# Small additions on GpSimd behind the gathers of adj, and an instruction order made from 16-byte ranges

## The chip, the cores and the metric

The kernel runs on one core of one Trainium2 chip. The metric is the device time of one execution in microseconds (us), as the median over several executions. Beside it there is a profile of one execution, taken by the hardware profiler. Its engines are TensorE (PE; its weight loads are PEld), VectorE (DVE), ScalarE (ACT), GpSimd (POOL) and SyncE (SP), which only issues transfers here.

## What is computed

Two layers of graph attention over 2708 nodes with 256 features. `adj` is 2708 x 2708, sparse, with non-negative entries and a full diagonal. Cut to what matters:

```python
# layer 0: sums over neighbours, three attention heads, two GRU cells
node_support = adj_without_diagonal @ h
edge_output  = gru_cell(node_support, h, edge_weights)
for each of 3 heads:
    hW = h @ W                        # e from sums of hW over the neighbours
    att = softmax over neighbours of e, masked where adj is 0
    edge_support += (att * adj_without_diagonal) @ hW
node_output = gru_cell(edge_support / 3, h, node_weights)
x = layernorm(x + diag * edge_output + diag * node_output)

# layer 1: four heads of 64
h = x @ W
e = leaky_relu(s_src[:, None] + s_dst[None, :]), kept where adj > 0.5
out = (softmax(e, axis=0)) applied to h, + bias
x = layernorm(x + out)
```

## The kernel before

The kernel doesn't multiply by the whole of `adj`. It looks once at all of it and makes lists of the rows in which a block of columns has entries; afterwards it gathers these rows alone.

**Scan (0 to about 200 us).** SP loads `adjT` in three parts of up to 1024 columns, 128 rows at a time. ScalarE takes signs, VectorE the marks of entries over 0.5, and TensorE packs those into bits. For each block of columns (`BLOCKS0`, 51 blocks of 28 to 64 columns) VectorE finds the rows with entries; `listed` turns that into indices `f_idx` through prefix sums on VectorE (arena `f_lists`) and small matmuls (`rk`, `lst`).

**Layer 0 (about 200 to 710 us).** Each block has 1 to 8 listed tiles of 128 rows, 131 in all. For each tile there are two gathers on GpSimd, both indirect DMAs through one column of `f_idx`: one takes the block's entries of these rows from `adjT` in DRAM (`fetch_raw`, into one of 40 slots of `f_raw`; the first 16 go into the space of `f_ah`), the other takes the rows of x with the head weights from the DRAM table `f_T0` (`fetch_rows`, into one of four `f_xg` buffers). Another 22 tiles are whole stretches of rows, which SP loads without a list. VectorE makes the weighted columns `f_four` out of both, TensorE sums into `acc`. Columns are worked in six groups of up to 512 (`CH`), in the order `turn`: 4, 3, 2, 1, 0, 5. When a group is summed, `cells_and_norm` runs its two GRU cells on TensorE (`side`), ScalarE and VectorE, normalises, and writes the table `f_T1` for layer 1. GpSimd adds twice for each block of 128 nodes (`f_xacc`, and the bias into `f_low`).

**Layer 1 (about 714 us to the end).** For the 32 blocks of `BLOCKS1` (96 tiles) GpSimd gathers rows of `f_T1` into the arena `f_lists` (`fetch_h`), VectorE masks and scales them, TensorE sums, and each finished block of 128 nodes is normalised and stored (`finished`). The lists for layer 1 are made by the same `listed`, in the same arena, before.

**What sets the order.** The program's calls are not issued as they are written. Each call goes to an object `Order` (lines 88 to 375), which keeps it as a node, or several calls as one node where `together()` encloses them. `issue` (line 223) finds the dependences: `spans` (line 134) gives, for each operand, the ranges of bytes of a partition that it touches, in cells of 32 bytes (1024 in DRAM, a whole bank in PSUM), and two nodes that touch a common cell, one of them writing, are kept in their order. `duration` (line 180) gives each call a price in us. From these a list scheduler works forwards and backwards twelve times and keeps the order with the shortest planned span. All instructions are then issued from line 375, in that order, so nearly every row of the profile says L375; each engine works its own instructions in the order given. A name that begins with `in_` (an input in DRAM) makes no dependence. The prices and cells are the planner's alone: they change which instruction comes when, not what it does.

Gathers are issued by `gathered` (line 812), from `fetch_raw` (line 841), `fetch_rows` (line 1063) and `fetch_h` (line 1344). A gather has the price 1.36 us in `duration`.

Of the kernel before, what the change touches and what calls it, by code (L numbers as in the profile page):

```python
# [14 lines left out]
U32 = mybir.dt.uint32  # L15
# [7 lines left out]
P = 128  # L23
# [49 lines left out]
def _size(ap):  # L73
    n = 1
    for d in ap.shape[1:]:
        n *= d
    return n


def _width(dt):  # L80
    return {F32: 4, I32: 4, U32: 4, BF16: 2, F16: 2, U16: 2, F8: 1}[dt]
# [6 lines left out]
class Order:  # L88
# [44 lines left out]
    @staticmethod  # L133
    def spans(ap):

        name, pat, wide = ap.tensor.name, [tuple(d) for d in ap.ap], _width(ap.dtype)
        if name.startswith("in_"):
            return name, []
        space = str(ap.space)
        if "PSUM" in space:  # L140
            return name, [(0, 1)]
        if "DRAM" in space:
            at, cell = ap.offset, 1024
        else:
            step = pat[0][0]
            at, cell = (ap.offset % step if step else ap.offset), 32
            pat = pat[1:]
        run, outer = 1, []
        for s, n in sorted((abs(s), n) for s, n in pat if s and n > 1):
            if s <= run + cell // wide:  # L150
                run = s * (n - 1) + run
            else:
                outer.append((s, n))
        starts = [at]
        for s, n in outer:
            starts = [a + k * s for a in starts for k in range(n)]
        out = []
        for a in sorted(starts):
            lo, hi = a * wide // cell, (a + run) * wide - 1
            hi = hi // cell + 1  # L160
            if out and lo <= out[-1][1]:
                out[-1] = (out[-1][0], max(hi, out[-1][1]))
            else:
                out.append((lo, hi))
        return name, out
# [14 lines left out]
    def duration(self, call):  # L180
        engine, method, args, kw = call
        outs, ins = self.touched(call)
        out = outs[0]
        n = max([_size(out)] + [_size(a) for a in ins if method in ("tensor_reduce", "bn_stats")])
        if engine == "tensor":
            moving = kw["rhs"] if method == "matmul" else args[1]
            still = kw["lhsT"] if method == "matmul" else args[1]
            cols = _size(moving) if method == "matmul" else P
            if _width(moving.dtype) == 4:
                if method == "transpose":  # L190
                    return 0.2
                return max(4 * cols + 2 * _size(still), 800 if _size(still) > 96 else 500) / 2400.0
            return max(cols, 108) / 2400.0 + 0.01
        if engine == "vector":
            wide = [a for a in outs + ins if _size(a) > 1]
            fast = all(_width(a.dtype) == 2 for a in wide) or (
                method == "tensor_scalar" and all("PSUM" not in str(a.space) for a in wide)
            )
            if method in ("tensor_tensor_scan",):
                n *= 1.5  # L200
            if method == "reciprocal":
                n *= 8
            if method in ("bn_stats", "tensor_reduce", "memset", "copy_predicated"):
                fast = False
            return ((n / 2 if fast else n) + 150 + (60 if method == "scalar_tensor_tensor" else 0)) / 960.0
        if engine == "scalar":
            extra = sum(isinstance(kw.get(k), bass.AP) for k in ("scale", "bias"))
            return (n + 224 + 93 * extra) / 1200.0
        if engine == "gpsimd":
            if method == "indirect_dma_start":  # L210
                return 1.36
            return (n * (4.0 if method == "tensor_add" else 0.8) + 60) / 960.0
        return 0.45

# [185 lines left out]
def fast_path(ctx: ExitStack, tc: tile.TileContext, i: dict, out: bass.AP, bad: bass.AP):  # L400
    nc = tc.nc
    R = Order(nc)
    V, S, G, T, Q = R.vector, R.scalar, R.gpsimd, R.tensor, R.sync
    x, xT_in, adj, adjT = i["x"], i["xT"], i["adj"], i["adjT"]
# [26 lines left out]
    def home(name, shape, dt=F32):  # L431
        return const.tile(shape, dt, name=name)
# [31 lines left out]
    T0 = dram.tile([N, TW0], F32, name="f_T0")  # L464
    T1 = dram.tile([N, TW1], U32, name="f_T1")
# [52 lines left out]
    G.iota(pos_i, pattern=[[P, NB]], base=0, channel_multiplier=1)  # L518
    spans = sorted({(b[2], NB) for b in BLOCKS0} | {(0, NB)})
    pos = home("f_pos", [P, len(spans), NB])  # L520
    past = home("f_past", [P, 1])
    V.tensor_scalar(past, pid, float(size[last]), 1.0e6, op0=ALU.is_ge, op1=MUL)
    for n, (lo, hi) in enumerate(spans):
        V.tensor_scalar(pos[:, n], pos_i, float(-P * lo), None, op0=ADD)
        if lo:
            V.memset(pos[:, n, :lo], 1.0e6)
        V.tensor_add(pos[:, n, last:], pos[:, n, last:], past)
# [53 lines left out]
    column = ({}, {})  # L581
# [9 lines left out]
    idx = [home(f"f_idx{l}", [P, wide_of[l]], I32) for l in (0, 1)]  # L591
# [7 lines left out]
    for l, blocks in enumerate((BLOCKS0, BLOCKS1)):  # L599
        at = l * slots_of[0]  # L600
# [208 lines left out]

    batch_part = [next(k for k, (lo, hi) in enumerate(parts) if lo <= BLOCKS0[b[0][0]][0] < hi) for b in batch0]  # L810

    def gathered(dst, table, ix, at):
        G.indirect_dma_start(dst, None, table, bass.IndirectOffsetOnAxis(ap=ix, axis=0), element_offset=at)

    work0 = []
    for n, (d0, w, q, room_) in sorted(enumerate(BLOCKS0), key=lambda e: (turn.index(e[1][0] // CH), e[0])):
# [16 lines left out]
    def raw_slots(a, b):  # L833
        if b <= early_n:
            return early[:, a:b]
        return raw_all[:, (a - early_n) % raw_n : (a - early_n) % raw_n + b - a]
# [4 lines left out]
    def fetch_raw():  # L841
        k = fetched[0]
        if k == len(work0):
            return False
        n, whole, t = work0[k]
        d0, w = BLOCKS0[n][:2]
        dst = raw_slots(k, k + 1)[:, 0, :w]
        if whole:
            with R.after(loads[1, 16]):
                Q.dma_start(dst, adjT[t * P : (t + 1) * P, d0 : d0 + w])  # L850
        else:
            gathered(dst, adjT, idx[0][:, column[0][n] + t : column[0][n] + t + 1], d0)
        raw_of[k] = dst
        fetched[0] += 1
        return True

    loads, known, seen = {}, [], []
    for g, (c0, c1) in enumerate(parts):
# [12 lines left out]
        for k in range(NB):  # L871
            p = size[k]
            at = at_ring.next()
# [47 lines left out]
    while fetched[0] < raw_n + early_n:  # L921
        fetch_raw()
# [39 lines left out]
    while s0 < len(BLOCKS1):  # L962
        n0 = by_slot[s0]
        d0, w = BLOCKS1[n0][:2]
# [13 lines left out]
    for c, cell in enumerate(("edge", "node")):  # L978
        pair = []
        for wn in ("Wih", "Whh"):  # L980
            t = wts.take([P, KD, 3 * D])
# [73 lines left out]
    while k < len(work0):  # L1055
        n, whole, t = work0[k]
# [6 lines left out]
    def fetch_rows(j):  # L1063
        ks = pairs0[j]
        n, whole, t = work0[ks[0]]
        if whole:
            return
        xg = xg_ring.next()
        for m, k in enumerate(ks):
            t = work0[k][2]  # L1070
            gathered(xg[:, m, :], T0, idx[0][:, column[0][n] + t : column[0][n] + t + 1], 0)
        rows_of[j] = xg

    def layer0(j):
# [188 lines left out]
    for j in range(ahead - 1):  # L1263
        fetch_rows(j)
    for g in turn:
        spread_dens(g)
        for j in steps[g]:
            if j + ahead - 1 < len(pairs0):
                with R.part(f"rows{BLOCKS0[work0[pairs0[j + ahead - 1][0]][0]][0] // CH}"):
                    fetch_rows(j + ahead - 1)  # L1270
            with R.part(f"sums{g}"):
                layer0(j)
            done = pairs0[j][-1] + 1
            check_raw(done)
            with R.part("raw"):
                while fetched[0] < min(max(checked[0], early_n) + raw_n, len(work0)):
                    fetch_raw()
        cells_and_norm(g)
# [65 lines left out]
    def fetch_h(j):  # L1344
        n, ts = work1[j]
        hg = hg_ring.next()
        for m, t in enumerate(ts):
            c = column[1][n] + t
            gathered(hg[:, m, :].bitcast(U32), T1, idx[1][:, c : c + 1], 0)
        hg_of[j] = hg  # L1350

    outs = {}
# [70 lines left out]
    for j in range(ahead1 - 1):  # L1423
        fetch_h(j)
    for j, (n, ts) in enumerate(work1):
        g = BLOCKS1[n][0] // CH
        if g + 1 < NG and g + 1 not in S_of:
            spread_values(g + 1)
        if j + ahead1 - 1 < len(work1):
            fetch_h(j + ahead1 - 1)  # L1430
        layer1(j)
# [455 lines left out]
```

## Time and profile before

| | us |
|---|---|
| three executions | 840.92, 841.58, 844.88 |
| median | 841.58 |
| the profiled execution, whole | 901.63 |
| its span, first to last instruction | 899.9 |

The profiled execution is slower than the others, so its microseconds are compared with its own total. In its span TensorE is busy 678.9 us, VectorE 551.1, GpSimd 436.2 and ScalarE 233.0. GpSimd's costliest groups:

| gathers | count | busy us | mean ns |
|---|---|---|---|
| adj's entries into `f_raw` | 115 | 116.2 | 1011 |
| adj's entries into `f_ah` (the first 16) | 16 | 16.1 | 1005 |
| rows of `f_T0` into four `f_xg` buffers | 131 | 138.6 | 1058 |
| rows of `f_T1` into `f_lists` | 96 | 108.6 | 1132 |

(The third row adds four groups: 39.1 + 34.7 + 34.7 + 30.1 over 36 + 33 + 32 + 30.) [...]In the profile's rows an arrow gives what is written on its left and read on its right, and "idle before" is the time in which the engine did nothing before an instruction, with what ended it: an engine and tile, a DMA, "issue" (nothing that the profile shows), or "remote", an unknown queue.

### The profile page before, as it was taken

What the parts mean: (1) busy time and instruction counts of PE and PEld (TensorE: products, weight loads), DVE (VectorE), ACT (ScalarE), POOL (GpSimd) and SP (SyncE); (2) the same over time, 40 slices, a digit from 0 to 9 for tenths busy, and PEclk for the clock granted to TensorE, in tenths of its full rate; (3) what the DMA queues carried; (4) which work ended last, traced back from release to release, by engine and by line L of the source; (5) the groups of instructions that cost most, each with busy time, mean ns of one, the idle gap of its engine ahead of it and who ended that gap; (6) DMA issues with size and microseconds to landing.
All of it is one profiled execution on the core that took longest, in us unless ns stands there. A gap on an engine that the chain in (4) does not pass through costs nothing. (4 is left out here: it accounts for less than half of the span.)

```text
span 899.9 us, 12878 instructions
## 1 busy us (share of the span) xinstructions
PE 678.9 (75%) x4588; PEld 481.8 (54%) x4588; DVE 551.1 (61%) x1355; ACT 233.0 (26%) x496; POOL 436.2 (48%) x565
## 2 busy tenths in 40 slices
PE   1474764778769899988898879999988565776664
PEld 1463653565335555565555545564467464765553
DVE  7373576695126847763436644561498734977996
ACT  4403664001011321122111121123125301113244
POOL 7006000476725716666677777550005266777830
PEclk9995555588979999999999999999999855787886
DMA  9934886572101312243223222121004244555541
GB/s 300 335 124 144 280 307 186 164 227 59 23 17 47 120 57 51 44 113 84 51 53 91 81 74 74 51 74 42 1 1 130 106 124 124 175 154 169 159 139 47
DMA packets 60647, 103.50 MB, mean 115 GB/s; under 512 B 20887, under 2 KB 37027, under 8 KB 59935
## 3 DMA queue, kind: packets, MB, share of 16 engines
q1 hardware_dynamic: 40337, 61.41, 20.5%
q0 software_dynamic: 17472, 41.15, 17.6%
q8 instruction: 38, 0.62, 0.3%
q10 hardware_dynamic: 2766, 0.04, 0.2%
q14 instruction: 34, 0.28, 0.1%
HBM read 93.07 MB, written 12.27 MB: 117 GB/s over the span
## 5 line engine op out<-in xcount | busy, mean ns | idle before, releaser
L375 POOL DMA_INDIRECT f_raw<-in_adjT_dram,f_idx x115 | 116.2, 1011 | 47.7 <-issue 31.9
L375 PE MATMUL acc<-f_lists 128*65 128x128 f32 (+3 forms) x768 | 100.3, 303 | 51.7 <-DVE f_lists L375 37.9
L375 POOL DMA_INDIRECT f_lists<-f_T,f_idx x96 | 108.6, 1132 | 50.2 <-issue 20.6
L375 PE MATMUL side<-f_xT,f_wts 128*128 128x512 f32 (+1 forms) x288 | 123.0, 553 | 13.0 <-DVE f_big L375 11.9
L375 PE MATMUL side<-f_big,f_wts 128*128 128x512 f32 (+1 forms) x288 | 123.1, 553 | 9.5 <-ACT f_big L375 8.4
L375 PEld LDWEIGHTS acc<-f_lists 128*65 128x65 f32 x768 | 92.0, 189 | 58.4 <-DVE f_lists L375 42.6
L375 PEld LDWEIGHTS side<-f_big,f_wts 128*128 128x128 f32 x288 | 53.1, 194 | 64.4 <-issue 54.9
L375 POOL DMA_INDIRECT f_xg__133<-f_T,f_idx x36 | 39.1, 1085 | 99.5 <-DMA f_T<-f_E 71.6
L375 PEld LDWEIGHTS side<-f_xT,f_wts 128*128 128x128 f32 x288 | 51.0, 191 | 60.7 <-issue 43.3
L375 ACT ACTIVATE f_big<-f_wts 128x1024 fp8e4<-128x1024 f32 (+2 forms) x66 | 61.7, 952 | 48.3 <-DMA f_wts<-in_adjT_dram 39.8
L375 POOL TENSOR_TENSOR f_xacc<-f_xacc,f_low 128x256 f32<-128x256 f32 (+1 forms) x22 | 22.6, 1029 | 96.9 <-ACT f_low L375 96.1
L375 ACT ACTIVATE f_big<-side,f_biases 128x512 f32<-128x512 f32 (+1 forms) x48 | 30.4, 636 | 129.3 <-PE side L375 76.6
L375 DVE TENSOR_TENSOR f_big<-f_big 128x512 f32<-128x512 f32 (+1 forms) x48 | 30.4, 636 | 49.7 <-ACT f_big L375 42.8
L375 DVE TENSOR_SCALAR f_wts<-f_wts 128x1024 fp8e4<-128x1024 f32 (+1 forms) x66 | 43.2, 662 | 25.1 <-DMA f_wts<-in_adjT_dram 23.3
L375 PE MATMUL side<-f_big,f_gat_w 128*128 128x512 f32 (+1 forms) x144 | 56.1, 544 | 2.5 <-DVE f_s_d L375 1.6
L375 DVE TENSOR_TENSOR f_lists<-f_big,f_lists 128x512 f32<-128x512 f32 (+4 forms) x56 | 44.3, 791 | 21.3 <-PE acc L375 6.9
L375 PEld LDWEIGHTS <-f_big 128*128 128x128 fp8e4 x968 | 36.4, 103 | 34.2 <-issue 18.6
L375 POOL DMA_INDIRECT f_xg__135<-f_T,f_idx x33 | 34.7, 1052 | 36.9 <-PE acc L375 24.4
L375 PE MATMUL side<-f_pow,f_wts 128*128 128x8 bf16 x484 | 23.6, 170 | 37.1 <-DVE f_wts L375 35.6
L375 PEld LDWEIGHTS <-f_lists 128*32 128x32 f16 (+6 forms) x617 | 35.4, 134 | 27.1 <-DVE f_lists L375 17.2
L375 PE MATMUL lst<-f_lists 128*128 128x256 f16 (+4 forms) x285 | 37.5, 297 | 16.0 <-DVE f_lists L375 16.0
L375 DVE TENSOR_TENSOR f_lists<-f_iota,f_lists 128x2816 f16<-128x2816 f16 (+5 forms) x26 | 49.4, 1922 | 0.3
(244 smaller groups left out, 1208.2 us busy)
## 6 DMA issues: line engine op xcount, KB each, us to landing
f_wts<-in_adjT_dram SPq DMA_DIRECT2D x42, 512.0 KB
f_wts<-in_adjT_dram SPq DMA_DIRECT2D x21, 330.0 KB
f_big<-f_Rd SPq DMA_DIRECT2D x5, 1024.0 KB
f_big<-f_Sd SPq DMA_DIRECT2D x5, 1024.0 KB
f_T<-f_ah SPq DMA_DIRECT2D x21, 132.0 KB
f_X<-f_low SPq DMA_DIRECT2D x21, 128.0 KB
f_low<-f_X SPq DMA_DIRECT2D x21, 128.0 KB
out_dram<-f_big SPq DMA_DIRECT2D x21, 128.0 KB
```

The source lines that it names most:

```text
L375: getattr(getattr(self.nc, engine_), method)(*args, **kw)
```

## The change

There are four edits.

1. A tile `f_idle` of one partition and 128 elements of 4 bytes is made and set to zero. `gathered` puts each gather in a node of its own, and where the table is `adjT` it adds to the same node one addition on GpSimd, `idle + idle` into `idle`. Nothing else reads or writes that tile. The argument `l` that `gathered` now takes isn't used.
2. `spans` makes no dependence from names that begin with `f_idle`, as for inputs.
3. The cells of SBUF from which dependences are found are 16 bytes instead of 32.
4. In `duration` a gather costs 1.27 us instead of 1.36, and the addition 0.45; a gather of adj with its addition is thus one node of 1.72.

```diff
-        if name.startswith("in_"):
+        if name.startswith(("in_", "f_idle")):
             return name, []
...
-            at, cell = (ap.offset % step if step else ap.offset), 32
+            at, cell = (ap.offset % step if step else ap.offset), 16
...
             if method == "indirect_dma_start":
-                return 1.36
+                return 1.27
+            if outs[0].tensor.name.startswith("f_idle"):
+                return 0.45
...
-    def gathered(dst, table, ix, at):
-        G.indirect_dma_start(dst, None, table, bass.IndirectOffsetOnAxis(ap=ix, axis=0), element_offset=at)
+    idle = home("f_idle", [1, P])
+    G.memset(idle, 0.0)
+
+    def gathered(l, dst, table, ix, at):
+        with R.together():
+            G.indirect_dma_start(dst, None, table, bass.IndirectOffsetOnAxis(ap=ix, axis=0), element_offset=at)
+            if table is adjT:
+                for _ in range(1):
+                    G.tensor_add(idle, idle, idle)
...
-            gathered(dst, adjT, idx[0][:, column[0][n] + t : column[0][n] + t + 1], d0)
+            gathered(0, dst, adjT, idx[0][:, column[0][n] + t : column[0][n] + t + 1], d0)
...
-            gathered(xg[:, m, :], T0, idx[0][:, column[0][n] + t : column[0][n] + t + 1], 0)
+            gathered(0, xg[:, m, :], T0, idx[0][:, column[0][n] + t : column[0][n] + t + 1], 0)
...
-            gathered(hg[:, m, :].bitcast(U32), T1, idx[1][:, c : c + 1], 0)
+            gathered(1, hg[:, m, :].bitcast(U32), T1, idx[1][:, c : c + 1], 0)
```

## The prediction

> **What bounds the kernel now.** I read the busy row in slices first, then busy times by stage, then GpSimd's instructions in order of time, and last the chain of waits over the seam between the two layers. The page's slices:
>
> ```profile
> PE   1474764778769899988898879999988565776664
> DVE  7373576695126847763436644561498734977996
> POOL 7006000476725716666677777550005266777830
> ```
>
> Each digit is 22.5 us. TensorE is at 8 or 9 tenths from about 200 to 650 us (layer 0), and at 5 to 7 in layer 1, where VectorE is at 7 to 9. GpSimd looks like 6 or 7 tenths in layer 0, but that row leaves out what lies between its instructions. In order of time:
>
> ```profile
> 466.60 0.95 POOL L375 DMA_INDIRECT f_raw<-in_adjT_dram,f_idx  x1 [0.30 <-issue]
> 467.86 0.95 POOL L375 DMA_INDIRECT f_raw<-in_adjT_dram,f_idx  x1 [0.30 <-issue]
> 469.12 0.95 POOL L375 DMA_INDIRECT f_xg__133<-f_T,f_idx  x1 [0.31 <-issue]
> 470.08 0.73 POOL L375 TENSOR_TENSOR f_xacc<-f_xacc,f_low 128x256 f32<-128x256 f32 x1
> 470.77 1.41 POOL L375 TENSOR_TENSOR f_low<-f_low,f_bias_b 128x256 f32<-128x256 f32 x2
> 472.33 0.96 POOL L375 DMA_INDIRECT f_raw<-in_adjT_dram,f_idx  x1 [0.16 <-issue]
> ```
>
> Columns are start, duration, operation, and in brackets the idle time before it. The reader is to see three prices: a gather is 0.95 us; between two gathers stand 0.30 us; between a gather and an addition 0.01, and between an addition and the next gather 0.16. So a gather really takes 1.25 us of the queue. By stage:
>
> ```profile
> 352.00:470.00 118.00, 103.62 (x428) 65.60 (x427) 59.79 (x150) 23.18 (x56) 79.32 (x80) 0.96 0.27 67
> 470.00:530.00 60.00, 52.87 (x214) 36.26 (x213) 37.73 (x101) 12.30 (x30) 44.57 (x44) 0.94 0.31 81
> 530.00:606.00 76.00, 70.36 (x236) 42.67 (x235) 41.67 (x101) 15.98 (x32) 48.71 (x53) 0.98 0.25 68
> 606.00:714.00 108.00, 94.02 (x523) 59.50 (x521) 65.12 (x136) 37.32 (x88) 16.07 (x15) 0.98 0.17 56
> ```
>
> (busy us of PE, weight loads, DVE, ACT, POOL, then clock and DMA). Between 352 and 530 us TensorE is busy 156.5 of 178 us, GpSimd 123.9; adding the 0.30 us behind each of some 118 gathers makes about 159. Counting only the idle stretches over 0.30 us in the instruction list, less 0.30 each, GpSimd has 19.8 us free there, and 17.1 us between 530 and 606. TensorE and GpSimd are thus nearly balanced. The seam, by the chain of waits:
>
> ```profile
> 714.68 2.07 DVE f_lists L375 x2
> ...
> 717.35 2.54 PE lst L375 x22
> 719.89 1.82 issue
> 721.72 0.15 DVE f_hm L375
> 721.87 5.13 another core or an unknown queue
> ...
> 727.03 0.07 DVE f_idx L375
> ...
> 727.14 0.57 DVE f_lists L375 x2
> ```
>
> The last list of layer 1 is finished while the first gathers of layer 1 are already under way, and VectorE, which works in order, stands 5.13 us at the write of f_idx before the first masks (727.14) can go.
>
> **What the Trainium skill says.** GPSIMD Engine Reference, section 3.1 (elementwise accounting), puts a two-input addition at about 2.6 cycles per element plus a dispatch; the trace's 0.73 us for 256 elements agrees in size. SBUF — State Buffer, section "Who interferes with whom", says that a VectorE instruction with two SBUF inputs and a GpSimd instruction that reads SBUF block each other. The trace agrees: four f_xacc additions that take 0.73 us alone took 8.70 us from 674.47 on, beside VectorE's f_lists work. Perfetto Trace Analysis, section "GPSIMD Engine Instruction", advises timing GpSimd by the spacing of starts; that is done here.
>
> **The idle additions.** There are 131 gathers of adj (115 into f_raw, 16 into f_ah). Each is now followed by an addition of 128 elements on one partition, which no row shows. By the row for 256 elements (0.73 us, of which by the skill's 2.6 cycles at 1.2 GHz 0.55 is elements) I estimate 0.18 + 0.28 = 0.46 us. The step adds 0.01 + 0.46 + 0.16 and loses the 0.30 behind the gather: 0.33 us. Bounds: 0.1 us, if the addition is mostly dispatch like the small memsets (0.10 to 0.17 us: 0.01 + 0.13 + 0.16 - 0.30 is about nothing), and 0.54 us if VectorE blocks it as it does the others (f_xacc means 1.04 and f_low 0.84 against 0.73 and 0.70, so about 0.2 more). I take 0.33: 131 x 0.33 = 43 us of GpSimd. The addition depends on nothing and nothing reads it; the memset of its tile is one of 153. Behind each addition stand the next gathers in GpSimd's queue, and for the gathers of f_xg TensorE waits.
>
> Where this lies: the 17 gathers before 100 us have 71.6 us of idle time behind them (nothing). About 20 between 200 and 250 (7 us) stand before an idle stretch of 14 us at 249 (nothing). From 352 to 530 there are 63 in the list: 63 x 0.33 = 20.8 against 19.8 us free, so 1.0 late; from 530 to 606 there are 11, 3.6 against 17.1, which takes it up. If that cover were gone, 1.0 us would be late; I count +0.5. VectorE's blocked operations cost at most 0.46 us each, and it has idle time in this stage (59.8 busy of 118): nothing.
>
> **The new order.** Every engine's order is made from prices and dependences. The price of a gather falls from 1.36 to 1.27 us; the trace's spacing is 1.25, with means of 1.01 + 0.30 for f_raw and 1.13 + 0.30 for the layer-1 gathers. A gather of adj with its addition is priced 1.72 against my 1.58. So the planner now holds GpSimd to be a little fuller than it is in layer 0 and a little emptier in layer 1; gathers of adj lose rank where something else can go. No instruction is added to SP; its transfers keep their dependences, but their places can move.
>
> Ranges of 16 bytes can only take dependences away, never add one. Which: blocks of layer 0 whose width is a multiple of 4 but not of 8 (52, 60, 44, 28) end inside a 32-byte range of sa and z, so that neighbours' closing copies were kept in sequence; the four columns of f_rstd and f_nmr of a group are 16 bytes, so two neighbouring groups shared a range; in layer 1 eight finishing blocks shared one, now four. These are on ScalarE and VectorE, with small durations. With fewer dependences the planned span can usually be kept or shortened; on the chip it may go either way.
>
> What the order is worth is bounded by what it leaves idle. At the seam: 1.82 + 5.13 us on the chain with VectorE idle. If the last list is finished before the gathers that now stand in its way, the second gather (718.45) starts after the first at 715.8, lands about 3.1 us after its end (as those issued until 732.37 released VectorE at 735.46), so at 719.8, and the masks start near 719.5 to 720 instead of 727.14: -7.3 us, after which the matmuls at 728.22 are late next. A whole list is worth more: the first one after 652 us is 9.0 us of VectorE (0.33 + 0.35 + 0.84 + 0.94 + 1.83 + 3.08 + 1.62), done between 652 and 717 where VectorE is full, while
>
> ```profile
> 600.00:650.00 50.00, 49.45 (x137) 23.53 (x136) 14.80 (x32) 14.75 (x34) 5.96 (x8) 1.00 0.09 30
> 650.00:700.00 50.00, 40.66 (x314) 32.09 (x313) 43.25 (x79) 18.49 (x44) 11.74 (x8) 0.97 0.23 75
> ```
>
> VectorE is busy 14.80 of 50 us before and 43.25 of 50 after. A list pulled forward gains up to 9.0, one pushed back loses as much. I take the seam alone, -7.3, since it is the one stall that the edit's two levers (GpSimd's prices, fewer dependences) both touch.
>
> **Sum.** Against the profiled execution, 901.63 us (span 899.9 and 1.7 around it): +0.5 - 7.3 = -6.8, so 894.8. The median of the runs shown is 841.58, or 0.933 of that; -6.8 x 0.933 = -6.3, so 835 us.
>
> **Rivals.**
> - GpSimd becomes the bound (slower). Place: 352 to 530 us. Against 19.8 us free and 63 gathers it decides from 19.8 / 63 = 0.31 us per gather, and surely from (19.8 + 17.1) / 74 = 0.50, where the stretch until 606 has nothing left to give. At a blocked price of 0.44: 27.7 - 19.8 = 7.9 late, every f_xg gather behind it comes late, TensorE's closing cells of group 0 (603 to 665 us, 99% busy) move with it, and the order brings nothing: +7.4 in run time, 849 us. At 0.54: 14.2 x 0.933, 855 us. For it: the balance just shown. Against: TensorE's queue sets f_xg's pace (the long GpSimd idles there are waits for PE acc), and f_raw runs up to 40 tiles ahead.
> - The new order is worse: a list is pushed 9.0 us back: 850 us. For it: the planner knows nothing of the waits at f_idx (5.13 us), so it can't steer clear of them.
> - Seam and one list both gain: -7.3 - 9.0 + 0.5 = -15.8, times 0.933: 827 us. For it: VectorE's hole from 604 to 648.
> - The edit doesn't do what it says: the dependences taken away held nothing, the additions fill idle time, and the order comes out equal where it matters: 841 us. For it: the shared ranges named above are mostly on one engine, in sequence anyway.
>
> **How the numbers follow.** Seam alone 0.36, seam and list 0.16, no change 0.16, GpSimd bound 0.20, order worse 0.12. The predicted time is the likeliest's, 835 us; its own range is 829 to 838. Both signs hold much of the chance, so the range goes from 820 (seam, list and a little of the tail) to 854 (blocked additions), leaving out some 0.1 on either side. A measurement here tells about 0.5% (4.2 us) from no change: faster 0.52, same 0.16, slower 0.32.
>
> **What would show it.** Right: gather followed by addition at a spacing of about 1.58 us, no growth of TensorE's idle time from 352 to 606, and the masks of layer 1 starting less than 6 us after the first gather of layer 1 where it is now 12.6 (714.55 to 727.14). Wrong: additions of 0.6 us or more, f_xg gathers without a wait for PE acc and TensorE idle behind them, a layer 0 that ends later than the 665 us of group 0's cells; or a list of layer 1 that still holds VectorE after the first gathers. The forecast fails if the order is mostly chance, since then a gain at the seam is paid for elsewhere.

## The result and the profile after

The changed kernel takes 851.79 us (median of 14 runs, 847.12 to 855.91), the kernel before 844.78 us in the same set (14 runs). The ratio is 1.0121, with a 95% interval of 1.0088 to 1.0154: slower by 1.2%, where 0.8% faster was forecast (835 against 841.58).

The kernel before takes 842 to 845 us in the set of the result and in the first and third set of experiments, and 896 to 907 us in the second, fourth and fifth, like its profiled execution shown above (901.63). So a ratio is always taken within one set, and the profile after (852.62 us, span 850.7) is compared with the kernel before as profiled in the first set (run `e1_before_again`, 850.03 us, span 848.3).

The page of the changed kernel, busy time and slices of 21.3 us:

```profile
PE 668.7 (79%) x4588; PEld 475.3 (56%) x4588; DVE 555.4 (65%) x1355; ACT 227.9 (27%) x494; POOL 497.9 (59%) x697
...
PE   1588658599978998988979989688998578757662
...
DVE  7396778854578258554656444576388657869995
...
POOL 7003903885888127888888788883022477767520
```

And of the kernel before in the first set, slices of 21.2 us:

```profile
PE 668.0 (79%) x4588; PEld 478.3 (56%) x4588; DVE 552.0 (65%) x1355; ACT 233.1 (27%) x496; POOL 441.4 (52%) x565
...
POOL 7006100477775537857787788340022477876720
```

(Rows of the changed kernel say L377: it is line 375 of before, two lines further down.) GpSimd is busy 56.5 us longer and stands at about 8 tenths through most of the stage of the gathers; the other engines have the same work. By stage, with bounds at the first and last gather of `f_xg` and the first gather of layer 1 (stretch; then its length and the busy us of PE, weight loads, DVE, ACT, POOL; clock, DMA share, GB/s). Before:

```profile
0.00:153.00 153.00, 84.40 (x1512) 74.83 (x1513) 100.58 (x261) 68.48 (x84) 33.94 (x180) 0.73 0.74 247
153.00:554.00 401.00, 366.50 (x1622) 232.77 (x1619) 245.12 (x605) 80.38 (x181) 277.79 (x268) 0.94 0.32 85
554.00:670.00 116.00, 101.02 (x550) 64.39 (x548) 70.31 (x155) 40.69 (x97) 21.53 (x22) 0.98 0.18 58
670.00:848.30 178.30, 116.12 (x912) 106.28 (x912) 135.93 (x337) 43.55 (x134) 108.13 (x96) 0.70 0.48 139
```

After:

```profile
0.00:139.00 139.00, 83.19 (x1481) 74.59 (x1482) 100.44 (x259) 67.73 (x84) 44.33 (x198) 0.78 0.83 277
139.00:569.00 430.00, 381.98 (x1723) 239.83 (x1720) 249.69 (x625) 86.66 (x203) 326.69 (x380) 0.95 0.28 78
569.00:670.00 101.00, 89.47 (x478) 56.45 (x476) 69.35 (x137) 30.10 (x73) 26.39 (x24) 0.97 0.21 67
670.00:850.70 180.70, 114.11 (x914) 104.46 (x913) 135.90 (x337) 43.40 (x135) 100.45 (x97) 0.70 0.48 138
```

The reader is to see a small net made of large parts: 14 us gained in the scan, 29 lost in the stage of the gathers, 15 gained in the closing of layer 0, 2.4 lost in layer 1; together +2.4 us of span. (The medians differ by 7.0: the execution of before that was profiled took 850.03 us, where the median in the set of the result is 844.78.) GpSimd's order in the stage of the gathers, after (start, duration, operation, idle before):

```profile
440.51 0.96 POOL L377 DMA_INDIRECT f_raw<-in_adjT_dram,f_idx  x1 [0.16 <-issue]
441.49 0.39 POOL L377 TENSOR_TENSOR f_idle<-f_idle 1x128 f32<-1x128 f32 x1
442.04 0.96 POOL L377 DMA_INDIRECT f_xg__133<-f_T,f_idx  x1 [0.16 <-PE acc L377]
443.30 0.95 POOL L377 DMA_INDIRECT f_xg__133<-f_T,f_idx  x1 [0.31 <-issue]
...
448.58 1.33 POOL L377 DMA_INDIRECT f_raw<-in_adjT_dram,f_idx  x1 [0.30 <-issue]
449.94 1.32 POOL L377 TENSOR_TENSOR f_idle<-f_idle 1x128 f32<-1x128 f32 x1
451.41 0.96 POOL L377 DMA_INDIRECT f_raw<-in_adjT_dram,f_idx  x1 [0.16 <-issue]
```

Undisturbed, a gather with its addition takes 1.53 us of the queue (440.51 to 442.04) against 1.25 between two bare gathers (443.30 follows 442.04 by 1.26). At times the addition takes three times as long (1.32). On average it takes 0.53, by its row on the page:

```profile
L377 POOL TENSOR_TENSOR f_idle<-f_idle 1x128 f32<-1x128 f32 x131 | 69.0, 527 | 2.3
```

### The profile page after: what moved, and what is told of

It reads as the page before. It is cut to its first block, busy times and chain, and to the rows that moved or that the text cites. A ratio compares the mean times of both kernels' runs of the same rounds, so it can differ in the third digit from the quotient of the medians.

```text
span 850.7 us, 13045 instructions
## 1 busy us (share of the span) xinstructions
PE 668.7 (79%) x4588; PEld 475.3 (56%) x4588; DVE 555.4 (65%) x1355; ACT 227.9 (27%) x494; POOL 497.9 (59%) x697
## 5 line engine op out<-in xcount | busy, mean ns | idle before, releaser
L377 POOL DMA_INDIRECT f_raw<-in_adjT_dram,f_idx x115 | 121.8, 1059 | 34.6 <-issue 23.3
L377 PE MATMUL acc<-f_lists 128*65 128x128 f32 (+3 forms) x768 | 100.8, 303 | 45.0 <-DVE f_lists L377 35.3
L377 PE MATMUL side<-f_xT,f_wts 128*128 128x512 f32 (+1 forms) x288 | 124.5, 558 | 7.9 <-DVE f_big L377 7.0
L377 POOL DMA_INDIRECT f_lists<-f_T,f_idx x96 | 100.1, 1043 | 52.2 <-PE acc L377 21.4
L377 PEld LDWEIGHTS acc<-f_lists 128*65 128x65 f32 x768 | 91.7, 188 | 52.4 <-DVE f_lists L377 41.6
L377 PE MATMUL side<-f_big,f_wts 128*128 128x512 f32 (+1 forms) x288 | 120.8, 543 | 0.0
L377 PEld LDWEIGHTS side<-f_big,f_wts 128*128 128x128 f32 x288 | 52.6, 192 | 54.5 <-issue 54.4
L377 PEld LDWEIGHTS side<-f_xT,f_wts 128*128 128x128 f32 x288 | 51.9, 193 | 55.0 <-issue 44.1
L377 POOL DMA_INDIRECT f_xg__133<-f_T,f_idx x36 | 36.9, 1025 | 68.7 <-DMA f_T<-f_E 31.6
L377 ACT ACTIVATE f_big<-f_wts 128x1024 fp8e4<-128x1024 f32 (+1 forms) x66 | 61.6, 952 | 51.5 <-DMA f_wts<-in_adjT_dram 35.9
L377 POOL TENSOR_TENSOR f_idle<-f_idle 1x128 f32<-1x128 f32 x131 | 69.0, 527 | 2.3
L377 POOL TENSOR_TENSOR f_xacc<-f_xacc,f_low 128x256 f32<-128x256 f32 (+1 forms) x22 | 20.7, 940 | 74.7 <-ACT f_low L377 73.9
L377 ACT ACTIVATE f_big<-side,f_biases 128x512 f32<-128x512 f32 (+1 forms) x48 | 30.4, 634 | 118.1 <-PE side L377 118.1
L377 PE MATMUL side<-f_pow,f_wts 128*128 128x8 bf16 x484 | 24.2, 170 | 47.0 <-DVE f_wts L377 40.7
L377 PE MATMUL side<-f_big,f_gat_w 128*128 128x512 f32 (+1 forms) x144 | 57.9, 557 | 2.1 <-DVE f_s_d L377 2.1
L377 DVE TENSOR_TENSOR f_lists<-f_big,f_lists 128x512 f32<-128x512 f32 (+4 forms) x56 | 44.1, 789 | 23.5 <-DMA f_lists<-f_T,f_idx 18.9
L377 DVE TENSOR_SCALAR f_wts<-f_wts 128x1024 fp8e4<-128x1024 f32 (+2 forms) x66 | 47.4, 725 | 15.7 <-DMA f_wts<-in_adjT_dram 13.2
L377 POOL DMA_INDIRECT f_ah<-in_adjT_dram,f_idx x16 | 18.6, 1162 | 62.3 <-DVE f_rel L377 60.0
L377 DVE TENSOR_TENSOR f_big<-f_big 128x512 f32<-128x512 f32 (+1 forms) x48 | 30.2, 629 | 30.6 <-ACT f_big L377 29.9
L377 DVE TENSOR_TENSOR f_lists<-f_iota,f_lists 128x2816 f16<-128x2816 f16 (+5 forms) x26 | 49.5, 1918 | 0.3
L377 PEld LDWEIGHTS <-f_wts 128*128 128x128 fp8e4 x484 | 20.7, 107 | 50.5 <-DVE f_wts L377 43.1
L377 ACT ACTIVATE f_big<-acc,f_hm 65x128 f32<-65x128 f32 (+1 forms) x88 | 24.8, 354 | 88.0 <-PE acc L377 74.0
```

The lines of the kernel that those rows point to most:

```text
L377: getattr(getattr(self.nc, engine_), method)(*args, **kw)
```

## The experiments

The kernels ran in five sets; each ratio is to the kernel before in its own set. Three theories are named in the expectations. A: layer 0 waits for GpSimd's queue, so time put into it comes out at the end, one to one. B: the additions cost because they and VectorE's two-input operations block each other. D: which engine is late depends on whether the kernel before takes 843 or 900 us in the set. In the first set alone B stands for something else, that the new order is the cost and the additions lie in idle time; C is named where it is used. Where additions are "not issued", they are planned and priced as in the changed kernel and left out only when the instructions are written; they compute nothing that the output needs.

### First set: the two halves of the change apart

The kernel before again (no edit, `e1_before_again`):

> The kernel before, once more, for a second profile of it. Ratio 1.00 within 0.5%. If the profiled execution of 901.63 us was out of the ordinary, this one's span lies near 845 us, and layer 0 ends (last cells of group 5) well before the 706 us of the first profile; then shares and idle times of that profile were too generous. If it was ordinary for a profiled execution, the span is near 900 us again.

Measured: 847.03 us against 843.2, ratio 1.0022 (0.9991 to 1.0054). Two batches of the same program thus differ by up to 0.5%.

The additions on the order of before: every engine's instructions in the old sequence, and the 131 additions put in as the instructions are written.

```diff
                 getattr(getattr(self.nc, engine_), method)(*args, **kw)
+                if method == "indirect_dma_start" and args[2].tensor.name == "in_adjT_dram":
+                    for _ in range(1):
+                        self.nc.gpsimd.tensor_add(self.idle, self.idle, self.idle)
```

> The order of before on every engine, with 131 idle additions put behind the gathers of adj, and nothing else. Theory A (GpSimd becomes the bound of layer 0 and the additions are the cost): 1.010 or more, up to 1.02, since the old order doesn't know of them. Theory B (the order that the planner made is the cost, the additions lie in idle time): within 0.3% of before.

Measured: 882.66 us, ratio 1.0473 (1.0428 to 1.0518). The order of the changed kernel without its additions:

```diff
+                if method == "tensor_add" and args[0].tensor.name.startswith("f_idle"):
+                    continue
                 getattr(getattr(self.nc, engine_), method)(*args, **kw)
```

> The order of the changed kernel on every engine, with the 131 additions not issued. Theory A: at or below before, 0.985 to 1.000, and 1.2% or more under the changed kernel. Theory B: as slow as the changed kernel, 1.010 to 1.014.

Measured: 822.12 us, ratio 0.9746 (0.9705 to 0.9786). So the two halves pull apart, and each is several times what the sum gave it; the additions cost more than A gave, and the first set's B is refuted by both. In the profiles each engine's instructions come in the sequence of before in the one, and of the changed kernel in the other, but for three small instructions that start nearly together. The third part alone, cells of 16 bytes with the old prices:

```diff
-            at, cell = (ap.offset % step if step else ap.offset), 32
+            at, cell = (ap.offset % step if step else ap.offset), 16
```

> Before with cells of 16 bytes instead of 32 and nothing else: no additions, the old prices. The order differs from before in many places. Theory A: the sign is open, 0.99 to 1.01, chance alone. Theory B, if the finer cells are what spoils the order: 1.01 or more.

Measured: 848.46 us, ratio 1.0042 (1.0017 to 1.0068): the cells alone don't make the order better.

### Second set: more time, another kind of time, and the parts of the order

In this set the kernel before took 898.36 us. Two additions instead of one (`range(2)` in the edit above):

> Two idle additions behind each gather of adj instead of one, on the order of the kernel before. Theory A (GpSimd's queue time passes to the end one to one, in layer 0): the second addition costs its 0.39 us and about 0.02 of gap, since the idle time after an addition is already paid; 114 gathers of adj after the first ones x 0.41 = about 47 us more than the one-addition run, so 925 to 935 us, ratio 1.09 to 1.11. Theory B (what costs is that addition and VectorE block each other[...]): twice the excess of the one-addition run, ratio about 1.095 as well, but with VectorE's own operations longer by the same amount. Theory C (the first addition tipped the order over into a bad phase, after which nothing more is lost): ratio 1.04 to 1.06.

Measured: 958.93 us, ratio 1.0673 (1.0599 to 1.0746), below what A and B gave and above C. A memset of the same length in place of the addition:

```diff
-                        self.nc.gpsimd.tensor_add(self.idle, self.idle, self.idle)
+                        self.nc.gpsimd.memset(self.idle, 0.0)   # 330 elements
```

> In place of the idle addition a memset of one partition that reads nothing and is sized to occupy GpSimd for about as long (330 elements, about 0.39 us), on the order of the kernel before. Theory A (queue time alone): the same as with the addition, ratio 1.04 to 1.05. Theory B (blocking between GpSimd's two-input reads and VectorE's): most of the loss goes, ratio 1.00 to 1.015.

Measured: 886.04 us, ratio 0.9835 (0.9773 to 0.9897), which neither theory gave. The new prices with cells of 32 bytes, additions not issued, and then cells of 16 bytes with 1.27 us but without the planned addition:

> The order made with the changed kernel's prices (1.27 us a gather, 0.45 us behind each gather of adj) but with ranges of 32 bytes, and the additions not issued. If the prices make the better order: ratio 0.97 to 0.98, like the changed order without additions (0.9746). If the ranges of 16 bytes are needed beside them: 0.99 to 1.01.

Measured: 1.0009 (0.9981 to 1.0037).

> Ranges of 16 bytes and 1.27 us a gather, but no addition planned or issued. If the lower price of a gather is what improves the order: ratio 0.97 to 0.985. If it is the 0.45 us planned behind the gathers of adj alone, which holds these back behind the gathers of f_xg: 0.995 to 1.01, like the ranges alone (1.0042).

Measured: 1.0358 (1.0292 to 1.0424), outside both forecasts. Its stage of gathers takes 472.6 us, where that of before takes 436.0 in the profile at 901.63; why wasn't found.

Two profiles of the same program, one at 901.63 and one at 850.03 us, differ in the waits of VectorE and ScalarE that nothing in the profile ends. In the profiled execution of before at 901.63 us (engine, line, what it waited for, us, times, longest):

```profile
ACT f_big L375 <- issue: 67.7, 21, 12.8
ACT f_big L375 <- remote: 35.9, 7, 8.4
```

```profile
DVE f_idx L375 <- remote: 16.0, 3, 9.7
DVE f_big L375 <- remote: 15.7, 2, 8.8
```

And all of VectorE's of this kind at 850.03 us:

```profile
DVE f_four__137 L375 <- issue: 2.8, 1, 2.8
DVE f_lows L375 <- issue: 0.6, 1, 0.6
```

Summed over all rows that end with "issue" or "remote", ScalarE stood 121.9 us and VectorE 80.2 us at 901.63, and 0.7 and 3.4 us at 850.03. The profiles of the second, fourth and fifth set have 33 to 148 us of it on ScalarE, those of the first and third 0.5 to 0.7. What makes the engines stand isn't in the profile and wasn't found. That GpSimd waits for buffers while they stand, so that time put into its queue is partly covered, is theory D. This set doesn't show it: two additions cost 60.6 us here, and the memset made the kernel faster. A and B are told apart where the kernel before takes 842 us.

### Third set: additions, memsets and both halves side by side

The kernel before took 841.69 us.

> The memset of 330 elements behind each gather of adj, order of before, now side by side with the addition. GpSimd's spacing with it was 1.48 us (0.95 + 0.36 + 0.16), with the addition 1.51. Theory A (queue time): equal to the addition's ratio in the same set of runs within 0.7%. Theory B (blocking with VectorE's two-input operations): at least 3% below it. Theory D (the condition decides: where the kernel before takes about 900 us, TensorE and the other engines stall elsewhere for 50 us and cover the additions, where it takes about 843 they don't): both near 0.98 to 1.01 if before is at 900, both at 1.04 to 1.05 if it is at 843.

Measured: 868.02 us, ratio 1.032 (1.0248 to 1.0392).

> The additions behind the gathers of adj on the order of before, again. Theory A: 1.047 as in the first set, and the memset beside it the same. Theory B: 1.047, and the memset beside it near 1.01. Theory D: 0.98 to 1.02 if before is at 900 in the set, 1.047 if it is at 843.

Measured: 885.85 us, ratio 1.0491 (1.0419 to 1.0564). GpSimd's order with the memset:

```profile
440.34 0.95 POOL L375 DMA_INDIRECT f_raw<-in_adjT_dram,f_idx  x1 [0.30 <-issue]
441.29 0.36 POOL L378 MEMSET f_idle<- 1x330 f32 x1
441.81 0.95 POOL L375 DMA_INDIRECT f_raw<-in_adjT_dram,f_idx  x1 [0.16 <-issue]
442.76 0.36 POOL L378 MEMSET f_idle<- 1x330 f32 x1
443.29 0.95 POOL L375 DMA_INDIRECT f_xg__133<-f_T,f_idx  x1 [0.16 <-issue]
```

The spacing is 1.48 us, 0.23 more than between bare gathers; 114 gathers of adj lie in the stage, 114 x 0.23 = 26.2 us, and 868.02 - 841.69 = 26.3 (20.9 to 33.0 by the interval). By the medians queue time comes out one to one. By the profiles it is less: from the first to the last gather of `f_xg` before takes 400.8 us (first set), the memsets 418.1 and the additions 429.4 (`e2`) and 430.7 (`e10`). So two thirds of the queue time or all of it comes out; the runs don't settle which.

The addition costs 44.2 us, 17.8 more than the memset. Its spacing, 0.97 + 0.55 = 1.52 by medians, accounts for 114 x 0.27 = 31. By means it is 1.04 + 0.59 = 1.63 against 1.31 without, 114 x 0.32 = 36, where the memset's 1.51 gives 23. So 13 of the 17.8 us are seen as longer additions and gathers, and in the stage the additions take 11.3 and 12.6 us more than the memsets. The rest lies before it: in the profile of `e10` the scan ends 11.8 us later than in that of `e9` (164.3 and 152.5), which `e2` doesn't repeat (155.1). The intervals of the two ratios don't meet, so a difference is real; some 11 to 13 us of it go with the addition.

The clock explains a third of this at most. The granted clock of the whole profile is 0.911 with memsets and 0.854 with additions, but nearly all of this lies in the second part of the scan, which takes as long at either. Before (first set), and then with memsets:

```profile
67.00:153.50 86.50, 53.97 (x1210) 47.47 (x1211) 58.89 (x147) 47.84 (x53) 17.87 (x17) 0.53 0.74 239
```

```profile
66.00:152.50 86.50, 56.47 (x1221) 49.47 (x1220) 59.72 (x149) 47.45 (x53) 24.49 (x35) 1.00 0.75 239
```

From the first to the last gather of `f_xg` it is 0.94 with memsets and 0.93 with additions, and TensorE is busy 369.3 and 373.5 us. VectorE, which has the same work, is busy 245.5 us with memsets and 249.0 with additions (244.9 before). That agrees in kind with the Trainium skill, SBUF — State Buffer, section "Who interferes with whom", by which GpSimd instructions that read SBUF and two-input VectorE instructions block each other; the memset reads nothing. A asked for the two kinds within 0.7%, B for 3% between them, and it is 1.7: A holds for the larger part, and B, as the likeliest reason, beside it for the smaller.

The same 63 gathers of adj that the sum was made on (352 to 530 us there) lie here at 324 to 491 us without additions and at 343 to 530 with them. Before, in the first set:

```profile
324.00:491.00 167.00, 154.01 (x643) 101.25 (x643) 97.73 (x253) 37.75 (x90) 125.71 (x123) 0.96 0.31 78
```

With the additions, in the third:

```profile
343.00:530.00 187.00, 160.80 (x651) 104.11 (x650) 100.43 (x251) 37.70 (x90) 154.78 (x186) 0.94 0.28 70
```

The stretch grows by 20 us, 0.32 us for each gather. Counted in the instruction list as the prediction counted it, GpSimd has 7.1 us free in it before, not 19.8, and 6.4 with the additions. Most of it is waits for a slot of `f_raw` that VectorE has to read first, in that stretch of before:

```profile
POOL f_raw L375 <- DVE f_four__137 L375: 7.1, 3, 4.9
```

The idle time of TensorE grows from 13.0 to 26.2 us: its waits for `f_four` grow from 6.6 to 14.9, and VectorE waits longer for gathers that come late.

> The changed kernel's order without the additions, again. If the gain is in the order's first stage, where the first gather of f_xg starts 14 us earlier: 0.97 to 0.98 in any set of runs. If it is chance of one set: within 0.99 to 1.01.

Measured: 823.08 us, ratio 0.977 (0.9709 to 0.9831).

> The changed kernel itself in the same set of runs as its two halves. If the halves add (as logarithms): the product of the ratio of the additions on the old order and of the ratio of the new order without additions, within 1%: 1.02 by the first set's numbers, where 1.012 was measured.

Measured: 854.7 us, ratio 1.0136 (1.0073 to 1.0199). The product is 1.0491 x 0.977 = 1.025, 1.1% above it, a little more than the 1% asked; the halves nearly add, and the additions cost 854.7 - 823.08 = 31.6 us on the new order, 12.5 less than on the old one.

### Where the new order gains

In the first stage of before, the waits of GpSimd by what ended them (first set), and then of the changed kernel:

```profile
POOL f_xg__133 L375 <- DMA f_T<-f_E: 63.8, 1, 63.8
```

```profile
POOL f_xg__133 L377 <- DMA f_T<-f_E: 31.6, 1, 31.6
```

`f_T0` gets its last part from the scan, and the first gather of `f_xg` waits for that: it comes at 153.5 us before and at 139.4 after (137.4 and 139.8 in the two runs without additions). The stretch in which the orders part, before and then after:

```profile
60.00:80.00 20.00, 15.62 (x212) 13.74 (x210) 11.43 (x38) 6.31 (x8) 10.28 (x10) 0.70 0.26 73
```

```profile
60.00:80.00 20.00, 18.71 (x362) 16.65 (x362) 13.31 (x42) 11.12 (x14) 3.33 (x5) 0.92 0.78 281
```

The new order scans on where the old one makes the first lists: 362 small matmuls against 212, and transfers at 281 GB/s against 73. The first list is 9.5 us later for it (66.8 and 76.3 us to the first gather of adj), which costs nothing, since GpSimd waits for the scan anyway. An earlier first gather isn't a gain by itself: with the cells alone (`e4`) it comes at 146.7 us, but the stage of gathers is 5.9 us longer and ends at 553.4 as before (554.3). In the new order without the additions the stage keeps its length (399.2 us in `e3`, 400.8 before), and the 14 us stay.

The other gain goes with one list of layer 1. Its index is written by VectorE; the first of layer 1's, before and after:

```profile
607.74 0.18 DVE L375 TENSOR_SCALAR f_idx<-rk 128x32 int32<-128x32 f32 x1
```

```profile
559.82 0.18 DVE L377 TENSOR_SCALAR f_idx<-rk 128x32 int32<-128x32 f32 x1
```

The last gather of `f_xg` is at 554.3 us before and 568.7 after. So this list was made 53 us behind it and is now made 9 us ahead of it, in the time of the gathers, when VectorE is busy six tenths (249.69 of 430 us). The closing stretch from there to the first gather of layer 1 falls from 116 to 101 us.

Where this list stands can be read in any set, because it is a matter of the sequence. The list relative to the last gather of `f_xg`, by the profiles:

| cells | gather | 0.45 planned | list | kernel |
|---|---|---|---|---|
| 32 | 1.36 | no | 53 us behind | before, first set |
| 16 | 1.36 | no | 55 behind | `e4` |
| 32 | 1.27 | yes | 54 behind | `e7` |
| 16 | 1.27 | no | 52 behind | `e8` |
| 16 | 1.27 | yes | 9 ahead | changed kernel |
| 16 | 1.36 | yes | 41 ahead, a second one 16 | `e16` |

It takes the planned 0.45 us and the cells of 16 bytes together; the 1.27 isn't needed for it. Why neither alone moves the list wasn't tried.

The length of the closing stretch goes with these lists in all twenty profiles: 112 to 121 us with no list of layer 1 ahead of the last gather of `f_xg`, 101 to 103 with one, 89 with two (`e16`). It isn't the list's own work alone: TensorE, the busiest engine there, has 11.6 us less to do in the stretch (101.02 and 89.47), and of its products with `f_w1c` 24 lie in it instead of 39. Nor is a list ahead free by nature: in `e16` the stage of gathers takes 473.7 us, against 426.0 in `e15` of the same set, where no list stands ahead.

### Fourth and fifth set: time taken out of the queue

The kernel before took 906.5 us in the fourth set. All 44 additions of x1 on GpSimd left out, the order kept (so the stored x1 lacks its bias, and the column sums aren't made):

```diff
+                if engine_ == "gpsimd" and method == "tensor_add" and args[0].tensor.name.startswith(("f_xacc", "f_low")):
+                    continue
                 getattr(getattr(self.nc, engine_), method)(*args, **kw)
```

> The kernel before with the 44 additions on GpSimd left out (the column sums into f_xacc, and the bias added to x1 before it is stored), so the values of layer 0's output lack the bias and its mean; order and everything else as before. Theory A (GpSimd's queue is what layer 0 waits for): 16 of these additions lie between 427 and 530 us of an ordinary execution; their durations sum to 13.2 us, their gaps to about 2, and 11 gaps of 0.30 behind gathers come back: 12 us shorter, up to 16 with the eight at 273 to 284: ratio 0.981 to 0.986. If GpSimd's queue is only full because it is paced by TensorE: 0.997 to 1.003. If the kernel before is at 900 us in the set: 0.99 to 1.00.

Measured: 0.9977 (0.9935 to 1.0018), as given for a set at 900. The changed order without idle additions, and those 44 on VectorE:

```diff
+                if engine_ == "gpsimd" and method == "tensor_add":
+                    engine_ = "vector"
                 getattr(getattr(self.nc, engine_), method)(*args, **kw)
```

> The changed order without the idle additions, and the 44 additions of x1 issued on VectorE at their place in that order. Theory A: 10 to 14 us below the same order with them on GpSimd (0.977): ratio 0.96 to 0.966. If VectorE stands waiting for ScalarE at them, or needs the time itself: 0.975 to 0.985.

Measured: 1.0037 (1.0006 to 1.0068), above both forecasts. Two orders more, `e15` as `e7`, and `e16` as the changed kernel with 1.36 for a gather, both without additions:

> The changed prices (1.27, and 0.45 planned behind the gathers of adj) on ranges of 32 bytes, additions not issued: 1.0009 in a set where before took 898. If the new prices need the ranges of 16 bytes to give the better order: 0.995 to 1.01 in an ordinary set too. If the other condition hid their worth: 0.97 to 0.985.

Measured: 1.0024 (0.9995 to 1.0052).

> Ranges of 16 bytes and 0.45 us planned behind the gathers of adj, but 1.36 us for a gather as before; additions not issued. If the planned 0.45 us is what holds the gathers of adj back: 0.97 to 0.985, like the changed order without additions. If the order is chance of every detail: anywhere from 0.98 to 1.02, and unlike it.

Measured: 1.0014 (0.9986 to 1.0043).

All four lie between 904 and 906.5 us, whatever their order. The first two were tried once more, and before took 896.14 us:

> The kernel before with the 44 additions on GpSimd left out (column sums into f_xacc, bias added to x1), order as before. Where before takes about 843 us, theory A (GpSimd's queue is what layer 0 waits for): 12 to 16 us shorter, ratio 0.981 to 0.986; if the queue is full only because TensorE paces it: 0.997 to 1.003. Where before takes about 900: 0.9977 as in the fourth set.

Measured: 0.9965 (0.9932 to 0.9997).

> The changed order without the idle additions, the 44 additions of x1 on VectorE at their place. Where before takes about 843 us, theory A: 0.96 to 0.966; if VectorE stands at them waiting for ScalarE: 0.975 to 0.985. Where before takes about 900: 1.004 as in the fourth set.

Measured: 1.0036 (1.001 to 1.0062), both as in the fourth set.

Taking work from GpSimd's queue brings little or nothing in these two sets. Whether it brings 12 us where before takes 843 stays open, as does the worth of the orders of `e8` and `e16` there. The fastest version that ran is the changed order without the additions, at 0.9746 and 0.977 in two sets at 842 to 843 us; in its plain form it didn't run in a set at 900, and with the 44 additions on VectorE it isn't faster than before there.

## Why the prediction was wrong

**The step that failed first** is the cover in the sum: "63 x 0.33 = 20.8 against 19.8 us free, so 1.0 late; from 530 to 606 there are 11, 3.6 against 17.1, which takes it up", counted as "+0.5". The 19.8 us were read from an execution in which VectorE and ScalarE stood for reasons that the profile doesn't show, and GpSimd with them (four of the stretches counted, 7.9 us, end with "remote"). In the profile at 850.03 us there are 7.1, and they aren't cover: they are waits for buffers inside the loop of gathers, sums and buffers coming free, and 6.4 of them stay when the gathers come later, so that the stretch grows by 20 us and not by 1.0. The additions cost 39.5 and 44.2 us on the old order and 31.6 on the new one, where +0.5 was counted. The warning was on record: the profiled execution was 60 us longer than the runs shown. The prediction answered it with a factor of 0.933 on the whole, as if each stage had been stretched alike. But 35 of the 52 us more lie between the first and the last gather of `f_xg` and none in the closing stretch; most of it was idle time, and idle time was what the sum spent.

**The price of the addition** was right as a sum and off in its parts. Forecast: 0.01 + 0.46 + 0.16 - 0.30 = 0.33 us a gather. Measured: 0.32 over the 63 gathers named; the addition itself takes 0.39 undisturbed (0.43 on average on the old order, 0.53 on the new), and the rest is gathers that take a little longer beside it. The bound of 0.54 for a blocked step wasn't reached: spread over 131 gathers, the additions cost 0.30 and 0.34 us each on the old order and 0.24 on the new.

**The seven us before an idle stretch** (some 20 gathers between 200 and 250 us, counted at nothing) were covered in part. The places named hold 17 + 20 + 63 + 11 = 111 of the 131 gathers: 40 lie between 176 and 275 us there, so 20 had no term. The 17 in the scan cost about nothing, as forecast: from the first gather of adj to the first of `f_xg` it is 87.8 us with additions (`e2`) and 86.7 without. The first 40 gathers of `f_xg`, with 40 gathers of adj among them, take 122.0 us without additions and 128.6 with them (first set): 6.6 us of the 13 that 40 x 0.33 would make.

**The second step that failed** is the seam, "I take the seam alone, -7.3". VectorE's 5.13 us before the write of `f_idx` aren't there in the first set, where the same two instructions of before follow each other at once:

```profile
677.30 0.15 DVE L375 TENSOR_SCALAR f_hm<-side 64x4 f32<-64x4 f32 x1 [3.10 <-PE side L375]
677.54 0.17 DVE L375 TENSOR_SCALAR f_idx<-rk 128x8 int32<-128x8 f32 x1
678.34 0.43 DVE L375 TENSOR_TENSOR f_lists<-f_big,f_lists 128x256 f32<-128x256 f32 x1 [0.63 <-DMA f_lists<-f_T,f_idx]
```

The chain had named the releaser "another core or an unknown queue", which on one core should have raised the question. The changed kernel has the same seam: the first gather of layer 1 at 670.49, the masks at 678.86, 8.4 us against 8.0 before (670.38 to 678.34) and less than 6 forecast.

**The order as a whole** gained far more than 7.3 us, 21.1 and 18.6 in the two sets at 842 to 843, and elsewhere. The list pulled forward had been a rival ("A list pulled forward gains up to 9.0", in a rival at 0.16); it happened, and the closing stretch, with this and other work gone from it, shrank by 15. The scan's 14 us were in no part of the prediction, though the page showed GpSimd idle for 71.6 us behind `f_T<-f_E`: the stage was read as time in which additions are free, not as time that an order could shorten.

**The rival that came true** is GpSimd as the bound (at 0.20, 849 to 855 us), with its place right. Its deciding point of 0.31 us a gather was made with the same 19.8; with 7.1 it is 0.11, and the measured 0.32 lies far beyond it. Its price, 7.4 to 13 us, was a sixth to a third of the additions' cost on the old order, again for the 19.8 us; and it assumed that "the order brings nothing". That 851.79 lies between its 849 and 855, and so inside the range up to 854, is luck. Two errors of opposite sign, of about 30 us in the additions and 14 in the order, leave the time 17 us above the forecast.

## What to carry to other kernels

When the profiled execution lies several per cent above the other runs, its idle times are the first thing not to trust: sum the waits of VectorE and ScalarE that end with "issue" or "remote", and spend no idle time of that execution as cover. An engine that waits for buffers inside a loop it feeds itself isn't free for that time: here 63 gathers with 0.32 us more each made their stretch 20 us longer. An order can be better for work that was planned and isn't done (18.6 and 21.1 us here): hold apart, by issuing one without the other, what an added instruction costs and what its planned place does to the order.

## What wasn't expected of the hardware

In the execution of 901.63 us VectorE and ScalarE stand for up to 9.7 and 12.8 us in the rows shown, and the profile names nothing of the program that holds them. In the second set, where before took 898.36 us, a memset of 0.36 us behind each gather of adj made the kernel before 1.65% faster (0.9773 to 0.9897), while in the third, at 841.69, it made it 3.2% slower; this stays unexplained.

A small addition on one partition takes 0.39 us of GpSimd undisturbed and up to 1.32 us in the lines shown. Between two gathers the queue stands 0.30 us; with an addition between them it stands 0.02 and 0.16, so the first 0.12 us of a small instruction in that place cost no queue time.
